# Attention in strips of 32 tokens on TensorE's column tiles, queries turned together with the attention weights, and list scatters and first gathers two in a sub-block

## The chip, the core and the metric

The kernel runs on one core of one Trainium2 chip. A core has five engines that run side by side and meet at semaphores: TensorE (PE; matmuls, with the loads of their stationary operand shown apart as PEld), VectorE (DVE), ScalarE (ACT), GpSimd (POOL) and SyncE (SP, which here issues nearly all plain DMAs). The metric is the device time of one execution in microseconds (us), the median of several runs.

## What is computed

Everything is float32. `x` has 4 batches of 1024 tokens of 256 values. Two residual steps follow each other. The first is cross attention with 16 heads of 64, in which the queries come from the normalised tokens and keys and values from 77 context rows of each batch:

```
q = layernorm(norm(x)) @ Wq;  q = q * (1 + scale) + shift
k, v = split(layernorm(ctx) @ Wkv)
x = x + softmax(q k^T / 8) v @ Wout
```

The second is a mixture of 9 experts of width 704, of which each token uses the two with the highest router probability, their weights normalised to a sum of one:

```
probs = softmax(norm(x) @ Wr);  w, idx = top_k(probs, 2);  w = w / sum(w)
x = x + sum over the token's two experts e of  w_e * (silu(n @ Wg[e]) * (n @ Wu[e])) @ Wd[e],   n = norm(x)
```

## The kernel before

**Folding.** Ahead of the loop the kernel folds the weights. `g_sb[b]` (256 x (16 x 77 + 9)) holds the keys with Wq folded in, so that scores are one product of the normalised token with `g_sb`; nine more columns give the router's logits of the token itself. `u_sb[b]` holds the values with Wout folded in, as 10 chunks of 128 (head, key) rows by 265 columns: 256 outputs and 9 logits. The first 8 chunks (`NP`) hold the first 64 keys (`JA`) of all heads, two more (`NR`) the remaining 13.

**The attention loop.** The 4096 tokens are taken as 32 sub-blocks of 128 (`N_SUB`; 8 groups `g` of 4 sub-blocks `s`). The loop at the end of the tile function writes out by hand the order in which each engine gets its work. For a sub-block i:

- `query(i)` (ACT, L263) normalises 128 tokens into `z`, with a constant 1 in the last column, whose share of the product is a row of offsets. It is issued two sub-blocks ahead. `query_turn(i)` transposes z in two TensorE transposes (L272) into a PSUM tile `pz`, which ACT copies to `zT` (L274). It is issued one sub-block ahead.
- `scores(i, k)` for three PSUM banks k of 6, 6 and 4 heads (462, 462 and 317 columns): two accumulating matmuls each (L285) with a half of zT as the stationary operand, then the negated maximum of each head on DVE (`mx`, L289). `exponentials(i, k)` runs 16 exponentials on ACT (L300) that read the bank and sum up as they go. Each bank has one PSUM tile, which the next sub-block uses again.
- `attention_weights(i)`, one sub-block later: DVE divides by the sums and writes `an` (L322, L327), one tile of 128 tokens by 10 x 128 (head, key) columns.
- `weights_turn(i)`: DVE transposes `an` in squares of 32 x 32 (L341) into `anT`, and SP writes that to DRAM (`a_d`, L344, 640 KB). `weights_back(i)`: SP reads it back in four DMAs (L352, 160 KB each) so that the squares come to the right partitions and `aT(i)` holds (head, key) rows by tokens. There are two `aT` buffers and two `a_d`.
- `values(i)` (L361), three sub-blocks after the scores (`LAG` = 3): ten accumulating matmuls of 128 rows of aT by 265 columns of u_sb. The stationary operand is `aT[:, :, n]`, 128 tokens with a step of ten floats. Then `attended(i)` adds the residual on DVE (L369, L370).

In one pass of the loop, TensorE gets: scores(i, 0), query_turn(i + 1), scores(i, 1), scores(i, 2), values(i - 3). DVE gets in between: attention_weights(i - 1), the maxima, weights_turn(i - 1). SP gets the write of a_d(i - 1) in the middle of the pass and the readback of a_d(i - 1) at its end, behind whatever else the pass issued on SP's queue: `load_x` (L220), the residual's copy to the output (L927), the store of the normalised tokens `y` (L967), and near the end of the loop the first experts' weights in parts (L1344 to L1354).

**Routing.** Per group, with a few passes' delay, DVE picks two experts of each token (`choices`), TensorE counts places with two matmuls of 36 columns (`ranks`, L1017 and L1020), DVE turns them into row numbers (`places`), and POOL scatters the entries (token number and weight) to the experts' lists in DRAM with indirect DMAs (`scatter`, L1049): 8 in a group. For the first four groups (`G_EARLY`) places() issues each group's 8 scatters at once; later ones go out during the first expert blocks. When the first four groups' lists are there, `early_blocks` picks six blocks, and `fetch` issues at once the first two blocks' weights, the gathers of token numbers (`tokens`, four blocks) and of the tokens (`inputs`, two blocks with two gathers each; both L1361).

**Expert blocks.** After the loop 39 blocks follow, of 256 or 128 tokens each, gated up and down with TensorE matmuls of 256 or 128 columns (L1421, L1449, L1516). Blocks of kind "flex" and "quart" split the 128 tokens among two or four experts and use column tiles of 64 or 32 columns (L1486 and part of L1516): each tile's stationary operand has 32 or 64 columns and writes its own 32 or 64 partitions of the output. The last two sub-blocks' values and the last two groups' routing run inside the first expert blocks.

Of the kernel before, what the change touches and what calls it, by code (L numbers as in the profile page):

```python
# [21 lines left out]
def kernel(  # L22
# [43 lines left out]
    NA = KC * P  # L66
    DE = D + E
# [40 lines left out]
    a_d = [dram.tile([P, NA], F32, name=f"a_d{i}") for i in range(2)]  # L108
# [22 lines left out]
    BH = B // 2  # L131

# [65 lines left out]
    def open_attention():  # L198
# [4 lines left out]
        an_of.append(q.tile([P, NA], F32, name="an", bufs=1))  # L203
        for z in zs:
            nc.gpsimd.memset(z[:, D - 1 : D], 1.0)
# [6 lines left out]
        for an in an_of:  # L212
            nc.gpsimd.memset(an[:, H * JA :], 0.0)
# [45 lines left out]
    def query(i):  # L259

        g, s = divmod(i, NS)
        o, r, _ = zscale[g]
        nc.scalar.activation(  # L263
            zs[i % 2][:, : D - 1], xg[g][:, s, : D - 1], AF.Identity,
            bias=o[:, s : s + 1], scale=r[:, s : s + 1],
        )
# [8 lines left out]

    def scores(i, k):

        zT = zTs[i]
# [5 lines left out]
        for c in range(C):  # L284
            nc.tensor.matmul(  # L285
                psc[:, :w], zT[:, c, :], g_sb[i // NS // GPB][:, c, h * J : h * J + w],
                start=(c == 0), stop=(c == C - 1),
            )
        nc.vector.tensor_reduce(  # L289
# [26 lines left out]
    def attention_weights(i):  # L316
# [11 lines left out]
            an[:, H * JA :].rearrange("p (m w n) -> p n m w", w=W, n=N2)[:, :, :, :JR],  # L328
# [5 lines left out]
    Q = 32  # L334
    NQ = P // Q

    def weights_turn(i):


        turned = pools["qpool"].tile([P, NQ, Q, KC], F32, tag="anT", name=f"anT{i}", bufs=1)  # L340
        nc.vector.transpose(  # L341
            turned.rearrange("p q t k -> p q k t"), an_of[0].rearrange("p (k q t) -> p q k t", q=NQ, t=Q)
        )
        nc.sync.dma_start(out=a_d[i % 2], in_=turned.rearrange("p q t k -> p (q t k)"))  # L344

    def weights_back(i):

        aT = aTs[i] = pools["qpool"].tile([P, NQ, Q * KC], F32, tag="aT", name=f"aT{i}")
        there = a_d[i % 2]
        by_key = there.rearrange("(a i) (q m) -> q i a m", i=Q, q=NQ)  # L350
        for q in range(NQ):
            nc.sync.dma_start(out=aT[q * Q : (q + 1) * Q], in_=by_key[q])  # L352

    pos = {}

    def values(i):
        b = i // NS // GPB
        aT = aTs.pop(i).rearrange("p a (t k) -> p (a t) k", k=KC)
        po = pos[i] = mm_tile(f"po{i}")
        for n in range(KC):  # L360
            nc.tensor.matmul(  # L361
                po[:, :DE], aT[:, :, n], u_sb[b][:, n, :], start=(n == 0), stop=(n == KC - 1)
            )
# [17 lines left out]
    with ExitStack() as kvs:  # L381
# [407 lines left out]
        def context_values(k, new=mm_tile):  # L789
            n = k // 2 + k % 2 * N2  # L790
            pv = new(f"pv{n}")
            for c in range(C):
                nc.tensor.matmul(
                    pv[:, : B * J], wv_sb[:, c, n * P : (n + 1) * P], cT[:, c, :],
                    start=(c == 0), stop=(c == C - 1),
                )
# [217 lines left out]
    def ranks(g):  # L1014
        pp = routed[g]["pp"] = mm_tile(f"pp{g}")
        sel, cums = routed[g]["sel"], routed[g]["cums"]
        nc.tensor.matmul(  # L1017
            pp[:, : NS * E], before, sel.rearrange("p s e -> p (s e)"), start=True, stop=False
        )
        nc.tensor.matmul(  # L1020
            pp[:, : NS * E], ones, cums.rearrange("p s e -> p (s e)"), start=False, stop=True
        )

    def places(g):
# [7 lines left out]
        for k in range(2):  # L1032
# [4 lines left out]
            for s in range(NS):  # L1037
                pending.append((place_i, entries[k], s))
                if g < G_EARLY:
                    scatter()  # L1040
# [325 lines left out]
    def tokens(j):  # L1366

        nh, i, kind = blocks[j]
        while j == EARLY and pending:
# [6 lines left out]
        if j < EARLY:  # L1376
            apart(got, sent[2 * NS * G_EARLY :], "an early block's places are those of earlier groups")
            early_got.append(got)

    def inputs(j):  # L1380
        for h in range(blocks[j][0]):
            bound = TOK if j >= EARLY else G_EARLY * TB
            gather(of(yins, j)[:, h, :], y_d[:bound, :], ids[j][:, h, 0:1], bound)
# [190 lines left out]
    def fetch(in_parts=False):  # L1574
# [3 lines left out]
        for name, fn, lead in (  # L1578
# [8 lines left out]
            while ahead[name] < min(now[0] + lead + 1, end):  # L1587
                fn(ahead[name], in_parts) if name == "weights" else fn(ahead[name])
# [31 lines left out]
    N_SUB = NG * NS  # L1620
    LAG = 3
    chosen, early = None, None
    for i in range(N_SUB + 1):
# [7 lines left out]
        if now_on:  # L1631
# [4 lines left out]
            if 0 < i < N_SUB - 1:  # L1636
# [3 lines left out]
        if now_on and i:  # L1640
            scores(i, 1)
            exponentials(i, 1)
            extra(i, 1)
        if i > 0:
            weights_turn(i - 1)
# [8 lines left out]
        if now_on:  # L1654
# [4 lines left out]
            if i < N_SUB - 2:  # L1659
                query(i + 2)  # L1660
            if i:
# [37 lines left out]
        if early is not None:  # L1699
            if advance(early, 3 if sr == 3 else 9):  # L1700
                early = None
                now[0] = -1
                fetch(in_parts=True)
# [12 lines left out]
    for parts in partly:  # L1716
        advance(parts)

# [82 lines left out]
```

## Time and profile before

| what | us |
|---|---|
| median of 6 runs (lowest to highest) | 852.87 (852.47 to 854.28) |
| the profiled execution | 856.46 |
| its span, first to last instruction | 854.8 |
| attention loop's steady passes, 12 of them, 98.36 to 206.71 | 108.35 |
| DVE busy in 170.40 to 206.71 (36.31) | 33.18 |
| ACT busy in the same stretch | 29.48 |
| one transpose of the weights on DVE (L341) | 2.49 |
| one indirect DMA on POOL (L1049) | 1.06 |

The profile gives one execution's instructions by engine. A group of instructions is shown with its code line, engine, operation, the names of its output and inputs, their shapes, its count, its busy time, the mean time of one in ns, and the idle time before it with what ended that idle time. A matmul of float32 is recorded as two instructions, each with its weight load, and consecutive matmuls overlap, so their rate is read from start to start. Timeline lines give start, duration, engine and line. The queue of SP appears as SPq.

### The profile page before, as it was taken

What the parts mean: (1) busy time and instruction counts of PE and PEld (TensorE: products, weight loads), DVE (VectorE), ACT (ScalarE), POOL (GpSimd) and SP (SyncE); (2) the same over time, 40 slices, a digit from 0 to 9 for tenths busy, and PEclk for the clock granted to TensorE, in tenths of its full rate; (3) what the DMA queues carried; (4) which work ended last, traced back from release to release, by engine and by line L of the source; (5) the groups of instructions that cost most, each with busy time, mean ns of one, the idle gap of its engine ahead of it and who ended that gap; (6) DMA issues with size and microseconds to landing.
All of it is one profiled execution on the core that took longest, in us unless ns stands there. A gap on an engine that the chain in (4) does not pass through costs nothing. (4 is left out here: it accounts for less than half of the span.)

```text
span 854.8 us, 14468 instructions
## 1 busy us (share of the span) xinstructions
PE 842.5 (99%) x4148; PEld 676.4 (79%) x4148; DVE 596.6 (70%) x1887; ACT 380.1 (44%) x1570; POOL 311.1 (36%) x344
## 2 busy tenths in 40 slices
PE   8999999999999999999999999999999999999996
PEld 5755787787787788988888878788778878877895
DVE  4857788999999989544864575585578466667550
ACT  2778687978878697252222222222222222212221
POOL 3100000404233240377663453544444463453522
PEclk8999999999999999999999999999999999999999
DMA  8017566567665587896784799789679988788511
GB/s 292 3 50 223 161 175 204 172 188 219 181 185 168 172 263 226 285 321 135 202 246 129 199 337 353 207 240 336 176 222 346 302 218 284 216 247 251 120 21 19
DMA packets 129424, 177.25 MB, mean 207 GB/s; under 512 B 26167, under 2 KB 95295, under 8 KB 129216
## 3 DMA queue, kind: packets, MB, share of 16 engines
q1 hardware_dynamic: 111930, 158.57, 58.0%
q0 software_dynamic: 17344, 17.75, 11.4%
q8 instruction: 33, 0.54, 0.3%
q14 instruction: 47, 0.39, 0.2%
q10 hardware_dynamic: 70, 0.00, 0.0%
HBM read 136.89 MB, written 40.81 MB: 208 GB/s over the span
## 5 line engine op out<-in xcount | busy, mean ns | idle before, releaser
L1421 PE MATMUL pg<-xT,wgu 128*128 128x256 f32 x1100 | 242.7, 379 | 0.1
L1421 PEld LDWEIGHTS pg<-xT,wgu 128*128 128x128 f32 x1100 | 208.5, 190 | 28.7 <-ACT xT L1410 0.7
L1537 POOL DMA_INDIRECT out_dram<-co,ids x73 | 116.0, 1589 | 206.8 <-ACT co L1519 134.3
L300 ACT ACTIVATE ex<-psc,mx 128x77 f32<-128x77 f32 x512 | 159.1, 338 | 62.7 <-DVE mx L289 59.9
L1516 PE MATMUL po<-wd,hid 128*128 128x256 f32 (+2 forms) x768 | 173.2, 380 | 0.0
L1516 PEld LDWEIGHTS po<-wd,hid 128*128 128x128 f32 (+2 forms) x768 | 138.7, 183 | 28.6 <-issue 6.2
L1049 POOL DMA_INDIRECT list_d<-line,r_pli x64 | 67.8, 1059 | 234.4 <-DVE r_pli L1036 120.1
L361 PE MATMUL po<-u,aT 128*128 128x265 f32 x640 | 151.8, 392 | 0.0
L361 PEld LDWEIGHTS po<-u,aT 128*128 128x128 f32 x640 | 149.7, 311 | 2.6 <-ACT u L151 0.4
L1394 DVE STREAM_TRANSPOSE xT<-yin 32x128 f32<-32x128 f32 (+1 forms) x528 | 144.6, 274 | 9.0
L285 PE MATMUL psc<-g,zT 128*128 128x462 f32 (+1 forms) x384 | 146.7, 513 | 0.0
L1428 DVE TENSOR_TENSOR hid<-pg,sl 128x256 f32<-128x256 f32 x130 | 55.0, 424 | 117.5 <-ACT sl L1427 116.0
L1427 ACT ACTIVATE sl<-pg 128x256 f32<-128x256 f32 x130 | 49.7, 383 | 176.4 <-PE pg L1421 168.2
L300 ACT ACTIVATION_READ_ACCUMULATOR ex<-psc,mx 128x1 f32 x512 | 111.5, 218 | 0.0
L285 PEld LDWEIGHTS psc<-g,zT 128*128 128x128 f32 x384 | 69.7, 190 | 42.9 <-issue 34.4
L1519 ACT ACTIVATE co<-po,ids 128x256 f32<-128x256 f32 x66 | 31.1, 474 | 124.1 <-PE po L1516 121.6
L341 DVE STREAM_TRANSPOSE anT<-an 128x1280 f32<-128x1280 f32 x32 | 79.8, 2494 | 0.3 <-DMA a_d<-anT 0.2
L1361 POOL DMA_INDIRECT yin<-y_d,ids x66 | 69.2, 1048 | 24.3 <-issue 18.0
L289 DVE TENSOR_REDUCE mx<-psc 128x6 f32<-128x462 f32 (+1 forms) x96 | 53.7, 559 | 18.5 <-PE psc L285 18.5
L1506 DVE STREAM_TRANSPOSE hid<-hs 32x160 f32<-32x160 f32 (+1 forms) x112 | 39.5, 353 | 1.6
L322 DVE TENSOR_TENSOR an<-ex,rs 128x1024 f32<-128x1024 f32 x32 | 39.4, 1230 | 1.1
L1449 PEld LDWEIGHTS pt<-xT,wgu 128*128 128x128 f32 x308 | 35.1, 192 | 2.1 <-issue 2.0
(370 smaller groups left out, 769.8 us busy)
## 6 DMA issues: line engine op xcount, KB each, us to landing
wgu<-in_L_ffn_Wg_dram SPq DMA_DIRECT2D x33, 704.0 KB
wd<-in_L_ffn_Wd_dram SPq DMA_DIRECT2D x33, 640.0 KB
a_d<-anT SPq DMA_DIRECT2D x32, 640.0 KB
aT<-a_d SPq DMA_DIRECT2D x128, 160.0 KB
wgu<-in_L_ffn_Wu_dram SPq DMA_DIRECT2D x33, 512.0 KB
w_up<-in_L_ffn_Wg_dram SPq DMA_DIRECT2D x12, 704.0 KB
d_up<-in_L_ffn_Wd_dram SPq DMA_DIRECT2D x12, 640.0 KB
w_up<-in_L_ffn_Wu_dram SPq DMA_DIRECT2D x12, 512.0 KB
```

Source lines behind the costliest of these rows:

```text
L285: nc.tensor.matmul(psc[:, :w], zT[:, c, :], g_sb[i // NS // GPB][:, c, h * J : h * J + w], start=(c == 0), stop=(c == C - 1),)
L289: nc.vector.tensor_reduce(nmx[i][:, h : h + n], psc[:, : n * J].rearrange("p (h j) -> p h j", h=n), AX.X, ALU.max, negate=True,)
L300: nc.scalar.activation(exs[i][:, h + q, :], pscs[k][:, q * J : (q + 1) * J], AF.Exp, bias=nmx[i][:, h + q : h + q + 1], accum_out=sms[i][: ...
L341: nc.vector.transpose(turned.rearrange("p q t k -> p q k t"), an_of[0].rearrange("p (k q t) -> p q k t", q=NQ, t=Q))
L361: nc.tensor.matmul(po[:, :DE], aT[:, :, n], u_sb[b][:, n, :], start=(n == 0), stop=(n == KC - 1))
L1049: i = nc.gpsimd.indirect_dma_start(out=list_d[:, :], out_offset=bass.IndirectOffsetOnAxis(ap=place_i[:, s : s + 1], axis=0), in_=entry.bit ...
L1361: return nc.gpsimd.indirect_dma_start(out=dst, out_offset=None, in_=src, in_offset=bass.IndirectOffsetOnAxis(ap=offsets, axis=0), **kw,)
L1394: yield nc.vector.transpose(xT[q : q + Q].rearrange("p c (h t) -> p h c t", t=P)[:, :nh, :, a : a + Q], of(yins, j)[a : a + Q].rearrange(" ...
L1421: nc.tensor.matmul(pg[:, g, :], w[:, c, at : at + P], xT[:, c, :], start=(c == 0), stop=(c == C - 1),)
L1428: made = nc.vector.tensor_tensor(hid[:, f, :], pg[:, 1, :], sl, ALU.mult)
L1516: nc.tensor.matmul(po[rows, :D], hid[:, f, at], d[:, f, :], start=(f == 0), stop=(f == NF))
L1537: i = nc.gpsimd.indirect_dma_start(out=out_r, out_offset=bass.IndirectOffsetOnAxis(ap=ids[j][:, h, word : word + 1], axis=0), in_=cos[j][: ...
```

## The change

- A helper `strips` makes a product as four matmuls of 32 stationary columns each, on the four column tiles, with the same moving operand. It is used for the scores, the values, the ranks and most of the context's values; other products keep their form.
- `aT` has two more chunks (`KT` = 12). From sub-block 5 on (`RIDE`) ACT writes the normalised tokens of sub-block i + 3 into the last 256 columns of `an`, so that they are transposed on DVE, written to DRAM and read back together with the weights of sub-block i; scores(i + 3) takes its stationary operand from aT(i). Sub-blocks 0 to 4 keep the TensorE transposes.
- `anT` and `aT` hold chunks by tokens, with 32 tokens next to each other, where they held tokens by chunks.
- `places` only queues the scatters. `next_place` issues two in a pass, one after the second bank's maxima, one after the weights' transpose, each made to wait for that DVE instruction. When the first four groups' scatters are out, the first gathers go the same way (`first_fetch`): two blocks' token numbers, two blocks' tokens, two more blocks' token numbers. The first weights are issued in parts as before.

```diff
     NA = KC * P
+    KT = KC + C
+    Q = 32
+    NQ = P // Q
+    N_SUB = NG * NS
+    LAG = 3
+    RIDE = LAG + 2
     DE = D + E
...
     u_d = dram.tile([P, NP * DE], F32, name="u_d")
-    a_d = [dram.tile([P, NA], F32, name=f"a_d{i}") for i in range(2)]
+    a_d = [dram.tile([P, KT * P], F32, name=f"a_d{i}") for i in range(2)]
     list_d = dram.tile([ROWS, WORDS], I32, name="list_d")
...
+    def strips(out, left, right, **kw):
+        for a in range(0, P, Q):
+            nc.tensor.matmul(out[a : a + Q], left(a), right, **kw)
     def mm_tile(name):
...
         zs.extend(q.tile([P, D], F32, name=f"z{i}", bufs=1) for i in range(2))
-        an_of.append(q.tile([P, NA], F32, name="an", bufs=1))
-        for z in zs:
+        an_of.append(q.tile([P, KT * P], F32, name="an", bufs=1))
+        nc.gpsimd.memset(an_of[0][:, H * JA :], 0.0)
+        for z in zs + [an_of[0][:, NA:]]:
             nc.gpsimd.memset(z[:, D - 1 : D], 1.0)
...
                 nc.gpsimd.memset(t.bitcast(I32), NOWHERE)
-        for an in an_of:
-            nc.gpsimd.memset(an[:, H * JA :], 0.0)
...
         o, r, _ = zscale[g]
+        z = zs[i % 2] if i < RIDE else an_of[0][:, NA:]
         nc.scalar.activation(
-            zs[i % 2][:, : D - 1], xg[g][:, s, : D - 1], AF.Identity,
+            z[:, : D - 1], xg[g][:, s, : D - 1], AF.Identity,
             bias=o[:, s : s + 1], scale=r[:, s : s + 1],
...
+    def turned_query(i, c):
+        if i < RIDE:
+            return lambda a: zTs[i][:, c, a : a + Q]
+        return lambda a: aTs[i - LAG][:, a // Q, KC + c, :]
     def scores(i, k):
-        zT = zTs[i]
         h, n = banks[k]
...
         for c in range(C):
-            nc.tensor.matmul(
-                psc[:, :w], zT[:, c, :], g_sb[i // NS // GPB][:, c, h * J : h * J + w],
+            strips(
+                psc[:, :w], turned_query(i, c), g_sb[i // NS // GPB][:, c, h * J : h * J + w],
                 start=(c == 0), stop=(c == C - 1),
             )
-        nc.vector.tensor_reduce(
+        return nc.vector.tensor_reduce(
             nmx[i][:, h : h + n], psc[:, : n * J].rearrange("p (h j) -> p h j", h=n), AX.X,
...
         nc.vector.tensor_tensor(
-            an[:, H * JA :].rearrange("p (m w n) -> p n m w", w=W, n=N2)[:, :, :, :JR],
+            an[:, H * JA : NA].rearrange("p (m w n) -> p n m w", w=W, n=N2)[:, :, :, :JR],
             ex[:, :, JA:J].rearrange("p (n m) j -> p n m j", n=N2),
...
-    Q = 32
-    NQ = P // Q
     def weights_turn(i):
...
-        turned = pools["qpool"].tile([P, NQ, Q, KC], F32, tag="anT", name=f"anT{i}", bufs=1)
-        nc.vector.transpose(
-            turned.rearrange("p q t k -> p q k t"), an_of[0].rearrange("p (k q t) -> p q k t", q=NQ, t=Q)
-        )
-        nc.sync.dma_start(out=a_d[i % 2], in_=turned.rearrange("p q t k -> p (q t k)"))
+        turned = pools["qpool"].tile([P, NQ, KT, Q], F32, tag="anT", name=f"anT{i}", bufs=1)
+        made = nc.vector.transpose(turned, an_of[0].rearrange("p (k q t) -> p q k t", q=NQ, t=Q))
+        nc.sync.dma_start(out=a_d[i % 2], in_=turned.rearrange("p q k t -> p (q k t)"))
+        return made
...
-        aT = aTs[i] = pools["qpool"].tile([P, NQ, Q * KC], F32, tag="aT", name=f"aT{i}")
+        aT = aTs[i] = pools["qpool"].tile([P, NQ, KT, Q], F32, tag="aT", name=f"aT{i}")
         there = a_d[i % 2]
...
         for q in range(NQ):
-            nc.sync.dma_start(out=aT[q * Q : (q + 1) * Q], in_=by_key[q])
+            nc.sync.dma_start(
+                out=aT[q * Q : (q + 1) * Q].rearrange("i a k t -> i a (k t)"), in_=by_key[q]
+            )
...
         b = i // NS // GPB
-        aT = aTs.pop(i).rearrange("p a (t k) -> p (a t) k", k=KC)
+        aT = aTs.pop(i)
         po = pos[i] = mm_tile(f"po{i}")
         for n in range(KC):
-            nc.tensor.matmul(
-                po[:, :DE], aT[:, :, n], u_sb[b][:, n, :], start=(n == 0), stop=(n == KC - 1)
+            strips(
+                po[:, :DE], lambda a: aT[:, a // Q, n, :], u_sb[b][:, n, :],
+                start=(n == 0), stop=(n == KC - 1),
             )
...
             for c in range(C):
-                nc.tensor.matmul(
-                    pv[:, : B * J], wv_sb[:, c, n * P : (n + 1) * P], cT[:, c, :],
-                    start=(c == 0), stop=(c == C - 1),
-                )
+                w, kw = wv_sb[:, c, n * P : (n + 1) * P], dict(start=(c == 0), stop=(c == C - 1))
+                if k < 2:
+                    nc.tensor.matmul(pv[:, : B * J], w, cT[:, c, :], **kw)
+                else:
+                    strips(pv[:, : B * J], lambda a: w[:, a : a + Q], cT[:, c, :], **kw)
             src = pv[:, : B * J].rearrange("p (b j) -> p b j", b=B)
...
         sel, cums = routed[g]["sel"], routed[g]["cums"]
-        nc.tensor.matmul(
-            pp[:, : NS * E], before, sel.rearrange("p s e -> p (s e)"), start=True, stop=False
-        )
-        nc.tensor.matmul(
-            pp[:, : NS * E], ones, cums.rearrange("p s e -> p (s e)"), start=False, stop=True
-        )
+        for k, (w, what) in enumerate(((before, sel), (ones, cums))):
+            strips(
+                pp[:, : NS * E], lambda a: w[:, a : a + Q], what.rearrange("p s e -> p (s e)"),
+                start=(k == 0), stop=(k == 1),
+            )
...
                 pending.append((place_i, entries[k], s))
-                if g < G_EARLY:
-                    scatter()
...
         nh, i, kind = blocks[j]
-        while j == EARLY and pending:
+        while pending and (j == EARLY or len(sent) < 2 * NS * G_EARLY):
             scatter()
...
             early_got.append(got)
+        return [got]
...
             bound = TOK if j >= EARLY else G_EARLY * TB
-            gather(of(yins, j)[:, h, :], y_d[:bound, :], ids[j][:, h, 0:1], bound)
+            yield gather(of(yins, j)[:, h, :], y_d[:bound, :], ids[j][:, h, 0:1], bound)
...
-    def fetch(in_parts=False):
+    def fetch():
...
             while ahead[name] < min(now[0] + lead + 1, end):
-                fn(ahead[name], in_parts) if name == "weights" else fn(ahead[name])
+                got = fn(ahead[name])
+                if name == "inputs":
+                    advance(got)
                 ahead[name] += 1
...
-    N_SUB = NG * NS
-    LAG = 3
+    first_gathers = []
+    def next_place(behind):
+        if first_gathers and len(sent) >= 2 * NS * G_EARLY:
+            for got in first_gathers.pop(0)():
+                after(got, [behind], "gathers go out one by one")
+        else:
+            scatter(behind)
+    def first_fetch():
+        for j in range(LEAD):
+            weights(j, True)
+        for fn, j in ((tokens, 0), (tokens, 1), (inputs, 0), (inputs, 1), (tokens, 2), (tokens, 3)):
+            first_gathers.append(lambda fn=fn, j=j: fn(j))
+        ahead.update(weights=LEAD, inputs=LEAD, tokens=LEAD + 2)
     chosen, early = None, None
...
                 extra(i, 0)
-            if 0 < i < N_SUB - 1:
+            if 0 < i < RIDE - 1:
                 query_turn(i + 1)
...
         if now_on and i:
-            scores(i, 1)
+            next_place(scores(i, 1))
             exponentials(i, 1)
...
         if i > 0:
-            weights_turn(i - 1)
+            turned = weights_turn(i - 1)
+            if now_on:
+                next_place(turned)
         if 1 < i < 2 + B:
...
                 queries_logits(i)
-            if i < N_SUB - 2:
+            if i + 2 < RIDE:
                 query(i + 2)
+            if RIDE <= i + LAG < N_SUB:
+                query(i + LAG)
             if i:
...
                 now[0] = -1
-                fetch(in_parts=True)
+                first_fetch()
         elif partly and i < N_SUB - 1 and advance(partly[0], 1):
...
         advance(parts)
+    assert not first_gathers
```

## The prediction

> **What bounds the kernel now.** I read the page first (engine totals), then the groups of instructions with their shapes kept apart, busy time by stretch, and the timelines of TensorE and of SP's queue over single sub-blocks.
>
> ```profile
> span 854.8 us, 14468 instructions
> PE 842.5 (99%) x4148; PEld 676.4 (79%) x4148; DVE 596.6 (70%) x1887; ACT 380.1 (44%) x1570; POOL 311.1 (36%) x344
> 170.40:206.71 36.31, 36.31 (x142) 28.72 (x141) 33.18 (x92) 29.48 (x152) 10.05 (x15) 1.00 0.63 189
> ```
>
> The third line is four sub-blocks of attention: stretch, sum, then busy PE, PEld, DVE, ACT, POOL, granted clock, DMA share, GB/s. TensorE never waits there, at full clock; DVE is busy 33.18 of 36.31 us, 91%. So attention lasts as long as TensorE's work, with DVE close behind; what is saved on TensorE reaches the end unless another wait opens. The profiled execution took 856.46 us (span 854.8); the median of the runs shown is 852.87. I form differences in the profiled execution and apply them to the median.
>
> One sub-block on TensorE, from the start of one set of values to the next:
>
> ```profile
> 206.71 4.74 PE L361 MATMUL po<-u,aT 128*128 128x265 f32 x20
> 211.28 1.71 PE L285 MATMUL psc<-g,zT 128*128 128x462 f32 x4
> 212.83 0.38 PE L272 MATMUL pz<-ident,z 128*128 128x128 f32 x2
> 213.05 2.78 PE L285 MATMUL psc<-g,zT 128*128 128x462 f32 x8
> 215.67 4.74 PE L361 MATMUL po<-u,aT 128*128 128x265 f32 x20
> ```
>
> The period is 215.67 - 206.71 = 8.96 us: values 4.57, scores 1.55 + 2.62, the query's transposes 213.05 - 212.83 = 0.22. (A matmul here is two records. A few matmul records are missing, so I use starts.) Every fourth sub-block has ranks too and takes 9.4.
>
> **The change, TensorE's part.** The expert blocks already use 32-column tiles:
>
> ```profile
> 569.67 1.24 PE L1421 MATMUL pg<-xT,wgu 128*128 128x256 f32 x5
> 570.84 0.40 PE L1516 MATMUL po<-wd,hid 128*32 128x256 f32 x1
> ...
> 571.08 0.38 PE L1516 MATMUL po<-wd,hid 128*32 128x256 f32 x1
> ...
> 573.24 0.38 PE L1516 MATMUL po<-wd,hid 128*32 128x256 f32 x1
> ...
> 573.57 0.60 PE L1449 MATMUL pt<-xT,wgu 128*128 128x128 f32 x3
> ```
>
> Between 571.08 and 573.24 lie ten steps of four strips: 0.216 us per step of 256 columns. Whole matmuls of 256 columns step at the same 0.216 (five in 1.17 us before 570.84, the last one longer). Four strips thus cost what one whole matmul costs, no more and no less. The change of shape does cost: the last whole matmul before 570.84 began at 570.53, 0.31 us earlier instead of 0.216, and leaving takes 573.57 - 573.24 = 0.33. So about 0.1 us per change.
>
> Scores: no gain, already at 0.3875 per 462 columns. Values: 20 steps of 265 columns at 0.216 x 265/256 = 0.2236 are 4.47 us against 4.56 (4.57 above): 0.09 saved, the cost of weights read with a stride of 40 bytes. 32 x 0.09 = **-2.9 us**. Transposes go from 27 sub-blocks: 27 x 0.22 = **-5.9 us** (0.27 in the sub-blocks where z is late; bounds -5.9 to -7.3). Changes of shape: three transposes among strips in sub-blocks 2 to 4, the prelude, the early count, and in the first expert blocks two values and two ranks, each in and out: some 16 x 0.1 = **+1.6 us** (1 to 2). Ranks in strips: four steps of 36 columns at about 0.11 before; bounded by half and double, +-0.2 us in each of eight, taken as nothing. Sum: **-7.2 us**.
>
> **DVE and ACT.** Each transpose grows from 1280 to 1536 elements but its output becomes contiguous.
>
> ```profile
> L341 DVE STREAM_TRANSPOSE anT<-an 128x1280 f32<-128x1280 f32 x32 | 79.8, 2494 | 0.3 <-DMA a_d<-anT 0.2
> L1394 DVE STREAM_TRANSPOSE xT<-yin 32x128 f32<-32x128 f32 x304 | 91.9, 302 | 5.0
> L1394 DVE STREAM_TRANSPOSE xT<-yin 32x64 f32<-32x64 f32 x224 | 52.7, 235 | 4.0
> L361 PEld LDWEIGHTS po<-u,aT 128*128 128x128 f32 x640 | 149.7, 311 | 2.6 <-ACT u L151 0.4
> L285 PEld LDWEIGHTS psc<-g,zT 128*128 128x128 f32 x384 | 69.7, 190 | 42.9 <-issue 34.4
> ```
>
> L1394, with contiguous rows of 32, costs (302 - 235)/64 = 1.05 ns per element plus 168 ns; L341 costs 1.95. If the stride of ten floats is the reason, the new one takes 1536 x 1.05 + 168 = 1.78 us, 0.7 less; if the 128 partitions are, 1536 x 1.95 = 2.99 us, 0.5 more. Weight loads of the same size with and without that stride (311 against 190 ns) and L327 (208 elements into a stride of four floats: 535 ns, where 1.05 + 168 gives 386) put it on the stride, so I take 1.78. DVE then needs 33.2 - 4 x 0.7 = 30.4 of about 35 us: cover for all its other work. The Trainium skill, "SBUF - State Buffer", section "Door 1: The DMA port swizzle", says that accesses within one 16-byte line run at full rate and that each step to another line pays; it sides with the stride, and by it alone the sum would be this one. ACT loses the copies of zT (27 x 0.40 us) and issues the same queries.
>
> **The new wait.** Scores of sub-block i+3 now need what values of sub-block i needed: aT(i). Values came last in the sub-block, scores come first, so the due time moves forward by 4.4 us. Behind a waiting score on TensorE's queue stand all later scores and values, and DVE, ACT and the next transpose behind those. I compared, from the trace's DMA packets, when the last 1280-byte packet of each aT(i) landed with the start of the scores that will need it. Normally it is 2 to 4 us early. For i = 7, 11, 15, 19, 23 it is 0.64, -0.04, 0.37, 0.65, -0.33 us early (below nothing is late): there SP holds the readback behind the store of y, which waits for ACT.
>
> ```profile
> 200.71 0.34 SPq L344 DMA_DIRECT2D a_d<-anT  x1
> 205.21 0.34 SPq L967 DMA_DIRECT2D y_d<-y  x1
> 205.65 2.19 SPq L352 DMA_DIRECT2D aT<-a_d  x4
> ```
>
> Corrections: two periods shrink by 0.32 each (-0.64); the semaphore follows the last packet by 0.35 (as L344 to L352 shows); 512 packets of 1536 instead of 1280 bytes take 3.3 us x up to 1.2 (-0.2 to -0.66, taken -0.4); y is stored earlier, by the faster transpose and the missing zT copy (+0.4 to +1.4, taken +1.0). Slack becomes 0.25, -0.43, -0.02, 0.26, -0.7: stalls of **+1.2 us** (0 to 5, with the ends). Then i = 26, 27, 28, where the first expert weights (704 KB each) go ahead of the readback on SP's queue: -2.2, -2.6, -0.1 us. Following the queue with the earlier transpose, I get 1.2 us for aT(26) and 2.1 for aT(27), after which aT(28) has the 3.3 us back: **+3.3 us** (1.5 to 8).
>
> **The list scatters and gathers.** 32 scatters and 8 gathers, of about 1.05 us each on POOL, keep their number but wait for DVE, two per sub-block. Queued behind them on POOL are the entries' copies (L1008), for which DVE's L1011 waits: 2.1 us per sub-block fit into 8.6, cover from POOL's 10.05 busy of 36.31 (without it up to 1 us of DVE per group). In the trace the gathers' packets (298 to 312 us) stretch aT(26)'s readback from 3.3 to 5.0 us; taking them out of there is in the 1.2 above. First gathers end two sub-blocks before block 0's turn: nothing. The memset of `an` now stands before those of z on POOL: L213 takes 0.31 us, and ACT's first z ends 0.6 us after z's memsets, so it is covered; without cover 0.3 us once.
>
> **Sum**: -2.9 - 5.9 + 1.6 + 1.2 + 3.3 = -2.7 us; 852.87 - 2.7 = **850.2 us** (profiled execution: 853.8).
>
> **Rivals.** *No stall*: DVE's lead makes every aT early; -7.2 us, 845.7. For: DVE sets when aT is written. Against: the y store and the weights are on SP's queue whatever DVE does. 12%. *Readback becomes the bound*, slower: aT(11), aT(23) and those of 26 to 28 arrive at the late ends, 5 + 8 us of TensorE idle against 7.2 saved: +5.8, 858.7; it decides from 7.2 us of idle on, and its middle is 856. For: the three negative slacks. Idle also costs clock: in 6.00 to 10.00 us PE is busy 1.73 us at clock 0.72, and the next 4 us run at 0.50, though that was a cold start. 24%. *The transpose keeps 1.95 ns*: DVE then needs 33.2 + 2.0 = 35.2 us per group against TensorE's 35.0, and every aT lands about 1.2 us later relative to its scores: about +7, 860. For: no row with 128 partitions and contiguous output. 10%. *TensorE cannot be fed*: a sub-block has 10 x 16 + 6 x 16 = 256 loads and matmuls instead of 68, 33.8 ns each. Densest in the trace: the 96 strip matmuls and 96 loads of L1486 from 551.11 to 555.97, 25 ns each, but some of these may have been queued before. At 36 ns a sub-block takes 9.2 us, 27 x 0.6 = 15 us more than forecast: 865. 6%. The Trainium skill, "TensorE: Matmul & The Clock Gate", section "Step-by-step: what each phase is for", gives about 62 ns per matmul where its sequencer decodes them in microcode; by it a set of values would take at least 80 x 62 ns = 5.0 us and the kernel would be slower; the 96 matmuls of L1486 came every 51 ns, so the trace speaks against it.
>
> **How the numbers follow.** My forecast, 850.2, has 48%; its own range is 847.5 to 852.5. About 0.2% (1.7 us) is what a measurement can tell. Faster: most of the forecast's and the no-stall case, 0.50. Same: the forecast's upper end and the readback's lower, 0.18. Slower: 0.32. The range from 845 to 859 takes in the no-stall end and the readback rival's end.
>
> **What would show it.** Right: L341 near 1.8 us; L361 steps of 0.223; periods of 8.6 us; TensorE idle before L285, put down to aT's DMA, only once in four sub-blocks and twice to three times at 290 to 320 us. Wrong: L341 near 3 us; idle before most scores; strips stepping over 0.23; half clock after an idle stretch.

## The result, and the profile after

The changed kernel takes **855.53 us** in the median of 18 runs (853.62 to 857.43) against 852.88 us of the kernel before (38 runs). The ratio is 1.0028, with a 95% interval of 1.0022 to 1.0034: 2.65 us slower, small but clearly told. The likeliest forecast was 850.2; what came true is the rival in which the readback becomes the bound (855.53 lies near its middle, 856, by luck in part, as told below).

The profiled execution took 854.38 us. Its page and its groups of instructions (output and inputs, shapes, count, then busy us, mean ns, idle before and what ended it) have these lines:

```profile
span 852.7 us, 20858 instructions
PE 832.3 (98%) x7334; PEld 597.0 (70%) x7334; DVE 579.5 (68%) x1887; ACT 374.8 (44%) x1543; POOL 305.3 (36%) x345
L142 PE MATMUL po<-u,aT 128*32 128x265 f32 x2560 | 150.0, 386 | 1.3 <-DMA aT<-a_d 1.3
L142 PE MATMUL psc<-g,aT 128*32 128x462 f32 (+1 forms) x1296 | 118.9, 511 | 8.7 <-DMA aT<-a_d 4.9
L354 DVE STREAM_TRANSPOSE anT<-an 128x1536 f32<-128x1536 f32 x32 | 56.6, 1769 | 0.0
```

TensorE is busy 10 us less than before (1.8 us of that lie ahead of values(2), where the execution profiled before ran at half clock for a while: 94.28 us busy there, 92.50 in e8 below). It idles ahead of scores (8.7 us) and values (1.3 us), which it did not do before. The profile puts 4.9 and 1.3 us of this down to the DMA that brings aT and most of the rest to instructions of DVE and ACT. The semaphore updates in the trace tell more: in each of the ten places the last update of a DMA that TensorE waits for there comes 0.13 to 0.35 us before it goes on. The transpose on DVE has fallen from 2494 to 1769 ns although it moves a fifth more.

Four sub-blocks, from one set of values to the fourth after it, in the windows view (start:end, sum, then busy PE, PEld, DVE, ACT, POOL, granted clock, DMA share, GB/s):

```profile
173.51:209.42 35.91, 34.94 (x532) 20.37 (x528) 31.08 (x93) 28.55 (x147) 8.43 (x11) 1.00 0.75 225
```

Before, four took 36.31 us and TensorE was busy in all of them. Now they need 34.94 us of work and last 35.91: in the steady part the change still gains, but only 0.4 us per four instead of 1.4.

One of the waits, on TensorE and then on SP's queue (start, duration, engine, line, what):

```profile
168.12 0.41 PE L142 MATMUL po<-u,aT 128*32 128x265 f32 x3
169.34 4.38 PE L142 MATMUL psc<-g,aT 128*32 128x462 f32 x48 [0.81 <-DMA aT<-a_d]
173.51 4.69 PE L142 MATMUL po<-u,aT 128*32 128x265 f32 x80
177.99 1.76 PE L142 MATMUL psc<-g,aT 128*32 128x462 f32 x16
```

```profile
157.75 0.34 SPq L355 DMA_DIRECT2D a_d<-anT  x1
162.38 0.34 SPq L983 DMA_DIRECT2D y_d<-y  x1
162.82 2.21 SPq L364 DMA_DIRECT2D aT<-a_d  x4
166.16 0.34 SPq L355 DMA_DIRECT2D a_d<-anT  x1
```

The values end, and the scores of sub-block 14 wait for aT(11). Its write to DRAM was issued at 157.75 and could have been read back from 161 us on, but the store of y, for which SP waits until ACT has written y (160.29 to 162.36), stands ahead of it, so that the readback starts at 162.82 and its last packet lands at 168.4. From here on idle time is counted from where the last step ought to have ended (its start plus the usual step), 0.16 us more than in the bracket: 0.97 us here.

The end of the loop, on TensorE:

```profile
306.76 4.38 PE L142 MATMUL psc<-g,aT 128*32 128x462 f32 x48 [1.91 <-DMA aT<-a_d]
310.93 4.69 PE L142 MATMUL po<-u,aT 128*32 128x265 f32 x80
317.14 4.38 PE L142 MATMUL psc<-g,aT 128*32 128x462 f32 x48 [1.52 <-DMA aT<-a_d]
```

These are the scores that need aT(26) and aT(27), whose readbacks stand behind parts of the first expert weights (`wgu`) on SP's queue:

```profile
296.29 0.42 SPq L1357 DMA_DIRECT2D wgu<-in_L_ffn_Wg_dram  x1
297.87 1.76 SPq L364 DMA_DIRECT2D aT<-a_d  x4
302.49 0.34 SPq L355 DMA_DIRECT2D a_d<-anT  x1
306.95 0.34 SPq L983 DMA_DIRECT2D y_d<-y  x1
307.50 0.39 SPq L1359 DMA_DIRECT2D wgu<-in_L_ffn_Wu_dram  x1
308.08 0.56 SPq L1360 DMA_DIRECT2D wgu<-in_L_ffn_Wu_dram  x1
308.83 0.42 SPq L1361 DMA_DIRECT2D wgu<-in_L_ffn_Wu_dram  x1
309.36 1.83 SPq L364 DMA_DIRECT2D aT<-a_d  x4
```

The packets of aT(26) run from 300.15 to 306.18, 6.0 us where earlier readbacks take 3.6 to 5.0; those of aT(27) end at 316.48.

Where the 2.65 us lie can be read by aligning the two executions at the start of values(2) and values(29). Before, that stretch lasts 240.67 us (339.03 - 98.36), after 242.28 us (335.30 - 93.02). TensorE idles some 10.5 us ahead of scores in it, so some 8.9 us of work went. From values(29) to values(31) it is 16.17 us before and 17.93 after, with 1.48 us of idle ahead of values(30) in the first expert block. From values(31) to the end the two agree: 499.57 and 499.46 us. The stretch ahead of values(2) is shorter by 1.1 to 1.6 us, if one takes for the kernel before an execution with an undisturbed start (below): in sum -1.3 + 1.6 + 1.8 = +2.1, against 2.65 in the medians.

### The profile page after: what moved, and what is told of

It is laid out like the page before. It is cut to its first block, busy times and chain, and to the rows that moved or that the text cites. A ratio compares the mean times of both kernels' runs of the same rounds, so it can differ in the third digit from the quotient of the medians.

```text
span 852.7 us, 20858 instructions
## 1 busy us (share of the span) xinstructions
PE 832.3 (98%) x7334; PEld 597.0 (70%) x7334; DVE 579.5 (68%) x1887; ACT 374.8 (44%) x1543; POOL 305.3 (36%) x345
## 5 line engine op out<-in xcount | busy, mean ns | idle before, releaser
L1062 POOL DMA_INDIRECT list_d<-line,r_pli x64 | 63.0, 984 | 250.2 <-DVE mx L305 168.8
L142 PE MATMUL po<-u,aT 128*32 128x265 f32 x2560 | 150.0, 386 | 1.3 <-DMA aT<-a_d 1.3
L142 PEld LDWEIGHTS po<-u,aT 128*32 128x32 f32 x2560 | 95.3, 110 | 51.6 <-issue 1.9
L142 PE MATMUL psc<-g,aT 128*32 128x462 f32 (+1 forms) x1296 | 118.9, 511 | 8.7 <-DMA aT<-a_d 4.9
L316 ACT ACTIVATION_READ_ACCUMULATOR ex<-psc,mx 128x1 f32 x512 | 107.2, 209 | 0.0
L142 PEld LDWEIGHTS psc<-g,aT 128*32 128x32 f32 x1296 | 47.4, 109 | 70.3 <-issue 54.8
L354 DVE STREAM_TRANSPOSE anT<-an 128x1536 f32<-128x1536 f32 x32 | 56.6, 1769 | 0.0
```

The source lines that it names most:

```text
L142: nc.tensor.matmul(out[a : a + Q], left(a), right, **kw)
L316: nc.scalar.activation(exs[i][:, h + q, :], pscs[k][:, q * J : (q + 1) * J], AF.Exp, bias=nmx[i][:, h + q : h + q + 1], accum_out=sms[i][: ...
L354: made = nc.vector.transpose(turned, an_of[0].rearrange("p (k q t) -> p q k t", q=NQ, t=Q))
L1062: i = nc.gpsimd.indirect_dma_start(out=list_d[:, :], out_offset=bass.IndirectOffsetOnAxis(ap=place_i[:, s : s + 1], axis=0), in_=entry.bit ...
```

## The experiments

Twelve runs. The first four ran beside each other on one chip, the next four on a second one, the last four on a third. Ratios are to the kernel before in the same runs.

**e1: the readback ahead of SP's other work.**

```diff
             values(d)
+        if 0 < i < N_SUB - 1:
+            weights_back(i - 1)
...
-        if 0 < i < N_SUB - 1:
-            weights_back(i - 1)
```

> The changed kernel with one statement moved: the four readback DMAs of the turned weights and queries are issued right after the values' matmuls, ahead of the stores and loads that the same pass puts on SP's queue (x, the residual's copy, y, the first experts' weights). Theory A (TensorE waits for a readback that SP's queue holds back): in the changed kernel's profile TensorE idles ahead of scores at 133.6, 169.3, 205.3, 241.1, 250.2 and 278.3 us (6.2 us in all) and at 306.8 and 317.1 us (3.75 us); all of that goes, about 9.9 us: 845.6 us, and passes stay at 8.65 us. Theory B (the DMA engines are too busy, order does not matter): the waits stay or move to the stores behind, gain under 2 us: 853.5 or more. Theory C (the strips themselves cost more than they save): no change, 855.5.

Measured: 865.6 us (862.34 to 865.97), ratio 1.0129 (1.0109 to 1.0148), much worse. SP's queue of this run:

```profile
306.03 0.65 SPq L355 DMA_DIRECT2D a_d<-anT  x1
313.74 1.75 SPq L364 DMA_DIRECT2D aT<-a_d  x4
315.59 0.38 SPq L983 DMA_DIRECT2D y_d<-y  x1
316.18 0.41 SPq L1359 DMA_DIRECT2D wgu<-in_L_ffn_Wu_dram  x1
...
318.58 0.45 SPq L355 DMA_DIRECT2D a_d<-anT  x1
```

SP now holds at the readback until the write has landed (306.03 to 313.74). The y store and the weights, which used that time before, follow it, and they are then in front of the next sub-block's write, which lands 10 to 14 us after the start of its pass (twice 18), where the change has 9.4 to 12.1. The wait moved from the readback to the write and grew: 17.7 us of idle in eleven places, against some 12.0 in all in the change, and by estimate 4.5 us more lost at half clock behind two of them. The longest, and the clock behind it:

```profile
320.60 7.18 PE L142 MATMUL psc<-g,aT 128*32 128x462 f32 x48 [3.56 <-DMA aT<-a_d]
```

```profile
320.30:323.20 2.90, 2.60 (x16) 0.91 (x20) 0.00 (x0) 0.00 (x0) 0.00 (x0) 0.50 1.06 375
```

48 strips take 7.18 us here and 4.38 elsewhere, since the granted clock is 0.50 after 3.7 us of idle.

**e2: only the store of y behind the readback.**

```diff
-        nc.sync.dma_start(out=y_d..., in_=y)
+        kept_back.append(lambda: nc.sync.dma_start(out=y_d..., in_=y))
+        if g == NG - 1:
+            kept_back.pop()()
...
             weights_back(i - 1)
+        while kept_back:
+            kept_back.pop()()
```

> The changed kernel with only the store of y put behind the readback of the same pass. Theory A: the idle stretches of every fourth pass go (1.33 + 0.97 + 1.14 + 0.80 + 1.49 = 5.7 us), those at 307 and 317 us stay, since the experts' weights are still ahead: 849.8 us. Theory B: under 1 us of gain, 854.5 or more. Theory C: 855.5.

Measured: 853.93 us (850.8 to 859.17), ratio 1.001 (0.9991 to 1.003), between the expectations. The median is 1.6 us better than the change's, but the two intervals overlap, so this gain is not told from noise; in the profiled executions the stretch from values(2) to values(29) takes 242.51 us, against 242.28. The readback of aT(11), without the store ahead, now lands 16.06 us after the start of the pass that made it instead of 17.41, that of aT(7) 15.51 instead of 17.98, and both are in time. But now aT(12), aT(20) and aT(24) are late, and 4.0 of 6.2 us of waits are left in the steady part. aT(12) lands no later in its pass than in the change (17.19 and 17.32 us); there the wait for aT(11) ahead of it had given it time. aT(20) and aT(24), with the store ahead of their writes, land 0.9 and 0.7 us later than in the change. At the end of the loop a wait of 2.38 us is followed by half clock: 32 strips in 4.96 us where 48 take 4.38.

```profile
324.53 4.96 PE L142 MATMUL psc<-g,aT 128*32 128x462 f32 x32 [2.22 <-DMA aT<-a_d]
```

So the y store ahead of the readback is the cause of the waits of every fourth sub-block, and with the store in another place in the queue most of the idle time stands one sub-block later.

**e3: scatters in bursts of eight and the first gathers at once, as before the change.**

```diff
                 pending.append((place_i, entries[k], s))
+                if g < G_EARLY:
+                    scatter()
...
     def next_place(behind):
-        ...
+        return
...
-            first_gathers.append(lambda fn=fn, j=j: fn(j))
+            list(fn(j))
```

> The changed kernel with the scatters of the first four groups issued in bursts from places() and the first gathers all at once, as before the change; strips and turned queries stay. If spreading them relieves the readback at the end of the loop, as the prediction had it (gather packets stretched aT(26)'s readback from 3.3 to 5.0 us), the idle stretches at 307 and 317 us grow by some 2 us in all: 857.5 us. If spreading does nothing: 855.5 us. If making POOL's DMAs wait for DVE costs something: under 855 us.

Measured: 858.49 us (856.39 to 860.42), ratio 1.0054 (1.004 to 1.0069), 3.0 us slower than the change. The wait for aT(23), beside which the bursts of scatters run, grows from 1.49 to 2.75 us, and that for aT(26), beside the gathers, from 2.07 to 4.56; both are followed by half clock. The second, and the clock behind it:

```profile
313.18 7.08 PE L142 MATMUL psc<-g,aT 128*32 128x462 f32 x48 [4.40 <-DMA aT<-a_d]
```

```profile
313.20:316.20 3.00, 3.00 (x16) 0.87 (x20) 0.00 (x0) 0.00 (x0) 1.99 (x2) 0.50 1.00 322
```

On the other side the waits for aT(27) (1.68 us) and ahead of values(30) (1.48) do not occur in this run, so idle time grows by less than 2 us, and the rest of the loss is time at half clock.

So spreading the scatters and gathers is worth 3 us, which the prediction had only as a share of one wait's 1.2 us. How the 3 us divide between scatters and gathers was not tried.

**e4: all queries turned on TensorE (strips, new layout and spread scatters stay).**

```diff
-    RIDE = LAG + 2
+    RIDE = N_SUB
```

> The changed kernel with RIDE = 32: all queries are transposed on TensorE, as before the change; strips, the twelve chunks of the transpose (the last two carry nothing that is used) and the spread scatters stay. No scores wait for a readback. Theory A: no idle stretches ahead of scores; a pass takes 8.65 + 0.22 for the transposes + 2 changes of shape of 0.1 = 9.07 us, so 27 passes are 0.11 us longer than before the change; in all 852.9 - 7.2 + 5.9 + 5.4 = 857.0 us. Theory B or C: idle time ahead of scores stays as it is, and 11 us more of transposes and changes of shape come on top: 866 us.

Measured: 859.76 us (857.78 to 860.75), ratio 1.007 (1.0055 to 1.0085). There is no idle ahead of any score, though the readbacks are as large as in the change: with the due time of before, all but the last two, for values(29) and values(30), are in time. But two whole transposes now stand between strips:

```profile
162.14 1.73 PE L142 MATMUL psc<-g,zT 128*32 128x462 f32 x16
163.80 0.44 PE L283 MATMUL pz<-ident,z 128*128 128x128 f32 x2
164.17 2.83 PE L142 MATMUL psc<-g,zT 128*32 128x462 f32 x32
```

A pass takes 9.155 us, 0.50 more than the change's 8.65: 0.22 for the transposes and 0.28 for two changes of shape, so 0.14 each, where the prediction took 0.1. Some 25 passes by 0.50 are 12.5 us; less the 10.5 us of waits that are gone, and with 2.8 us of idle ahead of values(29), that makes 4.8 us more than the change. The stretch from values(2) to values(29) is 4.3 us longer (246.60), the median 4.2. With whole transposes between them strips do not pay (a pass takes 9.155 us against 8.96 before); with the queries that ride they do, and that makes scores wait.

**e5 and e10: the queries ride four sub-blocks ahead instead of three.** Scores of sub-block i read aT(i-4), which landed a pass earlier; a new aT is first needed by its values, 4.4 us later in the pass. The third buffer for aT lies where the second tile of hidden values of the expert blocks will be. Since a query is written a pass earlier, `query_scale` also moves ahead of it in the pass, and three small tiles of the prelude get another place (both not shown in the cut diff).

```diff
-    RIDE = LAG + 2
+    AHEAD = LAG + 1
+    RIDE = AHEAD + 2
...
+    third = ctx.enter_context(tc.tile_pool(name="third", bufs=1, side="right")).tile(
+        [P, KT * P], F32, name="third"
+    )
...
-        return lambda a: aTs[i - LAG][:, a // Q, KC + c, :]
+        return lambda a: aTs[i - AHEAD][:, a // Q, KC + c, :]
...
-        aT = aTs[i] = pools["qpool"].tile([P, NQ, KT, Q], F32, tag="aT", name=f"aT{i}")
+        if i % 3 < 2:
+            aT = aTs[i] = pools["qpool"].tile(..., tag=f"aT{i % 3}", bufs=1)
+        else:
+            aT = aTs[i] = third.rearrange("p (q k t) -> p q k t", q=NQ, t=Q)
...
-        aT = aTs.pop(i)
+        aT = aTs[i]
...
-            if RIDE <= i + LAG < N_SUB:
-                query(i + LAG)
+            if RIDE <= i + AHEAD < N_SUB:
+                query(i + AHEAD)
...
+        hids.append(third.rearrange("p (f t) -> p f t", t=TS))
```

> Edit: a query rides four sub-blocks ahead of its scores instead of three (from the seventh query on), with a third buffer for aT, so that the scores of sub-block i read aT(i-4), which landed a pass ago. The first reader of a new aT is then its values, some 4.4 us later in the pass. Nothing is taken out: the same strips, transposes, write and four reads. Theory A (the loss is a due time: the scores ask for aT(i-3) at the start of the pass, and the readback of the sub-blocks that follow a y store comes 0.5 to 2 us after that): all idle ahead of scores goes, 6.2 us in the steady sub-blocks and 3.75 us at aT(26) and aT(27); 855.5 - 9.95 = 845.6 us (844.5 to 847.5), and the 1.5 us ahead of the values of sub-block 30 stays. Theory B (the queue of transfers is too full, so a later due time only moves the wait, as it did when the readback was put first): idle comes back ahead of the values, 852 us or more. Theory C (the wait on aT is not what costs; the time comes from slower strips): no change, 855.5 us.

**e6 and e11: the same, and the values of sub-block 30 later in block 0. e7 and e12: only that, in the changed kernel.**

```diff
-    in_first = {0: [lambda: late_values(N_SUB - 2)], 3: [last_values], 4: [lambda: turn(1)]}
+    in_first = {1: [lambda: late_values(N_SUB - 2)], 3: [last_values], 4: [lambda: turn(1)]}
```

> Edit: as e5, and the values of sub-block 30 are put behind the second instead of the first group of gate and up products of block 0. Theory A: the 1.5 us that TensorE idles ahead of these values go too: 845.6 - 1.5 = 844.1 us (843 to 846). Theory B: as e5 or no change to it, 852 us or more.

> Edit: only the values of sub-block 30 are put behind the second instead of the first group of gate and up products of block 0; all else as in the changed kernel. The idle time of 1.48 us ahead of them goes: 855.5 - 1.5 = 854.0 us (853.2 to 854.8). If that wait only hid another (the routing of the last group, which needs these values), no change, 855.5 us, or slower by up to 1 us.

**e8: the kernel before again.**

> The kernel before once more, with a profile: its first profile had a slow start (the clock at 0.50 from 10 to 14 us). Theory A: a profile with an undisturbed start has its start-of-values to end as the first one has, within 0.3 us, so that the changed kernel's loss lies between the values of sub-blocks 2 and 29 (240.7 us before, 242.3 us after). Rival: the 240.7 us were themselves out of the ordinary, by 1 us or more.

These four ran on a chip on which the kernel before takes 872.1 us. Measured there: e5 869.23 us, ratio 0.9975 (0.9952 to 0.9998); e6 868.69, 0.9965 (0.9947 to 0.9983); e7 876.21, 1.0052 (1.0029 to 1.0075). In e8 (872.33 us) the attention is what it was: values(2) to values(29) take 240.73 us (335.31 - 94.58) against 240.67, as its theory A said, and TensorE is busy throughout four sub-blocks; the chip loses its time from values(31) on, 519.1 us instead of 499.6.

```profile
170.57:206.90 36.33, 36.33 (x142) 28.74 (x142) 33.23 (x92) 29.54 (x153) 10.17 (x11) 1.00 0.64 192
```

In e5 there is no idle ahead of scores, but 4.1 + 2.5 us of idle inside the values ("issue" is time for which the profile shows nothing waited for):

```profile
L143 PE MATMUL po<-u,aT 128*32 128x265 f32 x1760 | 112.9, 387 | 4.1 <-issue 3.5
L143 PE MATMUL po<-u,third 128*32 128x265 f32 x800 | 52.4, 387 | 2.5 <-issue 1.9
```

so its stretch from values(2) to values(29) is 240.07 us. e7 had no changed kernel beside it and tells nothing by itself; the next four have it beside them.

**e9 to e12: on one chip, beside the changed kernel.**

> The changed kernel once more, beside e10 to e12 on one chip, because e5 to e7 fell on a chip on which the kernel before itself takes 872.1 us instead of 852.9 and on which the strips show idle spots of 0.25 to 0.5 us inside the values, that the first chip's profile of the changed kernel has none of. If the chip is like the first: ratio to before 1.0028. If it is like the second: 1.005, near e7's 1.0052, with such spots inside the values.

> e5 once more beside the changed kernel. Theory A (due time): faster than e9 by the idle ahead of scores, 9.95 us in the profile of the first chip, that is 845.6 us where before takes 852.9, ratio to before 0.9915; on a chip like the second some of it is lost inside the values and the ratio is e5's 0.9975, with e9 at 1.005 or above. Theory C (the wait on aT is not the cost): e10 equals e9 within 1 us.

> e6 once more. Theory A: e10 less 1.5 us, 844.1 us where before takes 852.9 (ratio 0.990). If the wait of these values only hid another one, the same as e10.

> e7 once more, now beside the changed kernel itself: e9 less 1.5 us if the 1.48 us idle ahead of the values of sub-block 30 is a loss by itself; the same as e9 or up to 1 us slower if it only hid the routing of the last group.

| run | us (lowest to highest) | ratio to before (95%) | values(2) to values(29), us |
|---|---|---|---|
| before | 853.11 (852.36 to 854.38) | 1 | 240.67, of its first profile |
| e9, the change | 855.7 (855.22 to 856.93) | 1.003 (1.0018 to 1.0042) | 243.17 |
| e10, queries a pass earlier | 848.02 (847.58 to 848.41) | 0.9937 (0.9924 to 0.9951) | 235.82 |
| e11, and values(30) later | 846.85 (846.48 to 847.91) | 0.9928 (0.9914 to 0.9941) | 235.13 |
| e12, only values(30) later | 854.7 (853.74 to 855.78) | 1.0016 (1.0007 to 1.0025) | 243.78 |

e10 is 7.7 us faster than the change with the same strips, transposes and transfers of the same size. What differs is the due time and the third buffer. That buffer could also have let readbacks start sooner, but they land no sooner: the last packets of aT(7), (11), (15), (19) and (23) come 18.2, 17.5, 17.5, 17.6 and 18.8 us after the start of the pass that made them in e10, and 18.1, 17.5, 17.4, 17.5 and 18.7 in e9. So it is the due time. Four sub-blocks of e9, then of e10:

```profile
174.35:210.01 35.66, 34.95 (x532) 20.86 (x528) 31.10 (x92) 28.54 (x147) 8.44 (x11) 1.00 0.75 221
```

```profile
171.75:206.48 34.73, 34.73 (x532) 18.41 (x528) 31.00 (x92) 28.42 (x148) 8.45 (x11) 1.00 0.78 228
```

TensorE is busy throughout e10's, as it was in the kernel before, with 34.73 us of work instead of 36.31. What is left of waits in e10 stands at the end of the loop, ahead of the values of the sub-blocks 27, 29 and 30:

```profile
312.67 4.69 PE L143 MATMUL po<-u,aT 128*32 128x265 f32 x80 [1.34 <-DMA aT<-a_d]
...
329.58 4.69 PE L143 MATMUL po<-u,third 128*32 128x265 f32 x80 [2.85 <-DMA third<-a_d]
...
336.88 3.34 PE L143 MATMUL po<-u,aT 128*32 128x265 f32 x56 [0.70 <-DMA aT<-a_d]
```

e9 idles 11.2 us ahead of scores and 1.4 ahead of values(30), e10 5.4 us ahead of these three sets of values (0.16 us above the bracket each): 7.2 of the 7.7 us. Beside the expert weights even the later due time is missed, and so not all came back that was expected; no run moved the weights, so that they are the cause is not shown. Theory A holds for the steady part, where nothing is left of the waits; what theory B describes, idle time coming back ahead of the values, happens in the last five sub-blocks, without its 852 us; theory C is out. Putting values(30) later gains 1.2 us in e11 and 1.0 us in e12, against the 1.5 expected. Each pair of intervals overlaps, but the traces agree: from values(29) to values(31) it takes 16.54 us in both, where e10 has 17.30 and e9 17.84. **e11 beats both kernels**, by 6.3 us the one before and by 8.9 us the changed one.

## Why the prediction was wrong, point by point

**The failed step is the term "stalls of +1.2 us" of the new wait.** The mechanism, the place and the sub-blocks of this term were right (aT(7), (11), (15), (19), (23), behind the y store), its size was not: these five waits measured 1.33, 0.97, 1.14, 0.80 and 1.49 us, with 0.49 more for aT(20), 6.2 us together (the bound was 5). The corrections to the slack were each too kind:

- The y store, taken 1.0 us earlier in the pass, came 0.5 earlier: 11.1 to 11.4 us after the start of the pass, where it was 11.6 to 11.9.
- The readback behind it, from first to last packet, was taken 0.4 us longer. It went from 3.2, 3.7, 3.4, 3.0 and 4.2 us to 4.5, 3.7, 4.0, 3.6 and 4.8: 0.6 longer in the mean, and up to 1.3.
- The lag from the last packet to the start of the scores, taken as 0.35 us from a write, is 0.6 to 1.1 us wherever TensorE was waiting (1.4 at aT(20)). Even behind a write the trace before has no less than 0.41 us, from the last packet to the issue of the readback.

0.5 + 0.2 + 0.5 is 1.2 us per sub-block. Against that the two periods shrank by 0.5 us in the mean and not by 0.64, which leaves 1.0 us, five times; that is the miss. A slack of 0.25 us was read as "no wait" when its own corrections were uncertain by more.

**Predicted by nothing**: 1.48 us ahead of values(30) in block 0.

**Right**: the tail in sum, 3.3 us forecast and 2.07 + 1.68 = 3.75 measured, though with 1.2 and 2.1 for its two parts. The transpose at 1.78 us (1.769). The pass at 8.6 (8.65). The mechanism of the rival that came true: TensorE waits for the readback by more than strips save.

**Luck**: that 855.5 lies at this rival's middle, 856. Idle time was 12.0 us, nearly the 13 of the rival's far end, and spread otherwise: over all five sub-blocks behind a y store, where the rival had aT(11), aT(23) and the tail. With the 7.2 us that it took as saved, this would be 857.7; that more work went (next paragraph) brought it back.

**TensorE's own share was larger than forecast.** The term of the ranks "taken as nothing", within 0.2 us, was outside its bounds: a sub-block with ranks took 0.45 us more than its neighbours before (9.40 against 8.95) and takes 0.13 more in e10 (8.78 against 8.65), 0.32 saved each time. For whole matmuls of 36 columns step at 0.11 us, and four strips of them together take about 0.03. The waits sum to 10.5 + 1.5 = 12.0 us and the kernel is 2.65 slower, so some 9.3 us of work went instead of 7.2. Eight ranks by 0.32 are 2.6 us, enough for this difference of 2.1; how the rest is made up was not worked out. The readback rival's turning point, 7.2 us of idle, was thus 9.3. In sum the forecast missed by 5.0 us at the y stores, 0.45 at the tail, 1.5 at values(30) and some 0.5 in smaller waits, less 2.1 of work: 5.3 us, the distance from 850.2 to 855.5.

**The rivals that did not come.** No stall (12%) is out with ten stalls in the profile, and the transpose at 1.95 ns an element (10%) with 1769 ns for 1536. That TensorE cannot be fed (6%) was wrong on the first and third chip, where values take 4.49 us per 160 loads and matmuls, 28 ns each. The Trainium skill, "TensorE: Matmul & The Clock Gate", section "Step-by-step: what each phase is for", has about 62 ns per matmul for decoding in microcode; here the strips' matmuls came every 56 ns, so no run on these chips shows that limit. The row by which the prediction spoke against it was misread: L1486 has 48 matmuls and 48 loads from 551.11 to 555.97, a matmul every 101 ns and not every 51, which says nothing of such a limit. The strips of L1516 in the same trace do speak against it: 48 matmuls from 570.84 to 573.57, 57 ns each. On the second chip TensorE did stand still among strips: the set of values(31) took 14.0 us in e5 (352.00 to 366.01) and its strips came one by one, 0.7 us apart:

```profile
360.33 0.39 PE L143 MATMUL po<-u,aT 128*32 128x265 f32 x1 [0.34 <-issue]
361.02 0.38 PE L143 MATMUL po<-u,aT 128*32 128x265 f32 x1 [0.31 <-issue]
```

Such spots also stand in e8's expert blocks between 368 and 377 us, where there are no strips. What holds TensorE there stays open: for these strips the profile names nothing, and no run was made to find it.

**Not tried**: the new layout of aT with whole matmuls. The 0.07 us per set of values (4.56 to 4.49, forecast 0.09) is therefore not divided between strips and layout.

## What to carry to other kernels

When work is taken off an engine by letting its operand ride with another transfer, compare the new due time with the landing of every such transfer, and count as late whatever has less slack than its own corrections are uncertain by (here 1.0 us). If some are late, move the due time rather than the queue: one more buffer and a pass more lead brought back 7.7 us, where two ways of reordering the queue brought 1.6, within noise, and -10. Column tiles in strips cost nothing in this kernel's products of 265 and 462 columns as long as whole matmuls don't stand between them (0.14 us at each change).

## What the runs showed of the hardware

- **The clock after idle time.** Idle stretches of TensorE of 2.28 (once of twice), 2.38 and 2.75 us (twice) were followed by 3.4 us at half clock, part of which can lie in the idle time; those of 3.72 and 4.56 us by 6.8 us, of which 5.7 and 5.5 lie behind the idle time. Those up to 2.20 us in the change, e1, e2, e9 and e12 were not, but nor were 2.35 us in e11 and 3.01 us in e10. There is no single threshold in these runs. The Trainium skill, "TensorE: Matmul & The Clock Gate", section "What's actually happening", puts the fall at an idle window of about 3.4 us that runs freely; the runs agree that the outcome varies, and differ in the size, since 2.38 us was enough.
- **Small products gain most from strips**: the ranks' two products of 36 columns took 0.45 us as whole matmuls and take 0.13 as strips, where the values' products of 265 columns gained 1.5%, with the new layout together.
- **A DVE transpose into contiguous rows is faster than one into a stride**: 1536 elements contiguous take 1769 ns (1.15 ns each), 1280 elements into a stride of ten floats 2494 ns (1.95 ns each).
